# A four-layer network on one core: loading the next pair's first rows ahead, spacing the norm chains, and adding the last residual on VectorE

## The chip, the core and the metric

The kernel runs on one core of a Trainium2 chip. Its engines run side by side, each through its own list of instructions, and wait for one another by semaphores: TensorE (PE) multiplies matrices into PSUM, VectorE (DVE) and ScalarE (ACT) compute elementwise, GpSimd (POOL) does small work and issues DMAs, and SyncE (SP) issues nearly all DMAs. The metric is the device time of one execution in microseconds (us); lower is better.

## The reference

The input has 8 images of 64 channels and 128 x 128 pixels, all float32. Four layers follow, each a residual around a group-normalized input:

```python
x = x + _L0_conv_ref(_gn(x), L0_conv_w, L0_conv_b)
x = x + _L1_conv_ref(_gn(x), L1_conv_coef, L1_conv_scale_base, L1_conv_scale_sp, L1_conv_bias)
x = x + _L2_conv_ref(_gn(x), L2_conv_dw_w, L2_conv_dw_b, L2_conv_pw_w, L2_conv_pw_b, L2_conv_cv_w, L2_conv_cv_b)
x = x + _L3_conv_ref(_gn(x), L3_conv_embed_weight)
```

- `_gn` subtracts the mean and divides by the deviation over groups of 2 channels, for each image.
- Layer 0, the adder layer: each of 64 outputs is `relu(b - sum(|patch - w|))` over the 576 values of a 3 x 3 patch.
- Layer 1, the spline layer: per channel, `scale_base * silu(x) + scale_sp * spline(x) + bias`.
- Layer 2, the wavelet layer: a Haar transform, depthwise 3 x 3, 1 x 1 and 3 x 3 convolutions, an exact GELU, and the inverse transform.
- Layer 3, the quantizer: each pixel's 64 channels are replaced by the nearest of 512 code vectors.

## The kernel before, in words

Images are worked on in four pairs; the two images' channels fill the 128 partitions. A program that orders the instructions of every engine by its own estimate of time stands between this source and the engines; inside the adder layer the order on TensorE, ScalarE and VectorE is the one written.

**Adder layer** (`layer0`, L479 on). The image is cut into 4 chunks of 32 rows (`RA`), the 64 outputs into 4 groups of 16: 16 parts `p` for a pair. For each output the nine taps are computed as 128 x 4096 tiles `buf`: kind A by one ScalarE activation (L594), D by one VectorE operation (L596), C and T by further VectorE operations on the same buffer (L600), which cover two or three taps. TensorE sums every tile over the channels with eight matmuls (L663). Which kinds make up an output is written in `PLANS`, by what else runs beside. The tile buffers form a ring (`free`), 8 in the first pair and 7 later; one of them holds the chunk of x with a border (`load`, L506; normalized in place by `pad`, L518). Tiles are computed ahead as far as buffers are free. Two tiles are a *step*; `chores` lists what else is done at a step: channel sums and their way through DRAM (L537 to L559), the ReLU (`relu`, L568), the residual, which is eight DMAs of GpSimd that add x in flight (`residual`, L578), then statistics and eight stores (`finish`, L582).

**Beside it**: during the adder layer of pair n, layers 2 and 3 of pair n-1 are computed (`layer2_beside`, L941; `layer3_beside`, L1097), and in the last two parts the statistics of the next pair's input (`raw_stats`, L397). These are generators; each `yield` is a step. Layer 2 and layer 3 list their events by step number; layer 2 has 452 steps beside parts 0 to 7, layer 3 has 396 beside parts 8 to 13.

**Spline layer** (`layer1`, L670 on). It has no other layer beside it. A unit is 8 rows; `twice` (L683) loads it so that both halves of the partitions hold one image (`xd`). The per-channel scales `sb` and `zb` (L700 to L707) come from the layer's `mr` and the weights `l1w`.

**Normalization** (`group_norm_steps`, L427). `mr` holds mean and reciprocal deviation. Statistics are aggregated by VectorE (L458, L459), summed over channel pairs by a small matmul (L436, called at L460), used by VectorE for the variance (L462 to L466), summed again (L467), and turned into the reciprocal root by GpSimd (L471). `group_norm` (L418) runs the chain through at once: in front of the adder layer for the next input and for layer 2, and, with `by_tile`, between adder and spline layer. In layer 3 it runs at steps 0, 2 and 4 (L1176).

**Between layers.** At the end of the spline layer of a pair, `run` (L1194) first does the chain of the next input and that of layer 2, then enters `layer0`, which loads and normalizes its first chunk (`load(0)`, `pad(0)`, L638). At the end of the adder layer the ReLU of part 15 is followed by GpSimd's residual, the statistics, the chain, and the spline layer's scales. The last pair has no other beside its layers 2 and 3, which follow one after the other.

Of the kernel before, what the change touches and what calls it, by code (L numbers as in the profile page):

```python
# [21 lines left out]
P = 128  # L22
# [4 lines left out]
RA = 32  # L27
# [73 lines left out]
class Net:  # L101
# [295 lines left out]
    def raw_stats(self, pair, stats):  # L397

        with self.tc.tile_pool(name="raw", bufs=3) as pool:
            for j in range(NCH):  # L400
                t = pool.tile([P, R * W], F32, name="raw")
                self.nc.sync.dma_start(out=t, in_=self.x_dram[pair][:, j * R * W : (j + 1) * R * W])
                yield
                self.tile_stats(stats, 4 * j, t)
                yield

# [11 lines left out]
    def group_norm(self, stats, by_tile=False):  # L418


        with self.tc.tile_pool(name="gn_ps", bufs=1, space=PSUM) as pp:
            mr = self.small.tile([P, 2], F32, name="mr", tag="mr", bufs=4)
            for _ in self.group_norm_steps(stats, mr, pp, by_tile):
                pass
        return mr

    def group_norm_steps(self, stats, mr, pp, by_tile=False):  # L427
# [6 lines left out]
        def product(lhsT, rhs):  # L434
            t = pp.tile([P, 2 * NG], F32, name="gn", tag="gn")
            nc.tensor.matmul(t[:, 0 : rhs.shape[1]], lhsT, rhs, start=True, stop=True)  # L436
            return t
# [21 lines left out]
        nc.vector.tensor_reduce(total, mv[:, :, 0], AX.X, ALU.add)  # L459
        pm = product(self.pair, total)  # L460
# [5 lines left out]
        nc.vector.tensor_reduce(total, dv, AX.X, ALU.add)  # L466
        pv = product(self.pair, total)  # L467
# [10 lines left out]

    def layer0(self, pair, mr, stats, bufs, beside):  # L479

# [7 lines left out]
        with ExitStack() as ctx:  # L488
# [4 lines left out]
            free = deque(bp.tile([P, (RA + 2) * (W + 2)], F32, name=f"buf{n}") for n in range(bufs))  # L493
            held, xps, pss, sums, sxs, sts, ys = {}, {}, {}, {}, {}, {}, {}
            plan = [beside(p)[0] for p in range(NP)]

            def rows(j):

                lo, hi = max(j * RA - 1, 0), min((j + 1) * RA + 1, H)
                return lo, hi, xps[j][:, lo - j * RA + 1 : hi - j * RA + 1, 1 : W + 1]  # L500
# [5 lines left out]
            def load(j):  # L506
                held[j] = free.popleft()
                xp = xps[j] = held[j].rearrange("p (r w) -> p r w", w=W + 2)
                nc.gpsimd.memset(xp[:, :, 0:1], 0.0)
                nc.gpsimd.memset(xp[:, :, W + 1 : W + 2], 0.0)  # L510
                if j == 0:
                    nc.gpsimd.memset(xp[:, 0, 1 : W + 1], 0.0)
                if (j + 1) * RA == H:
                    nc.gpsimd.memset(xp[:, RA + 1, 1 : W + 1], 0.0)
                lo, hi, at = rows(j)
                nc.sync.dma_start(out=at, in_=x_in[:, lo * W : hi * W].rearrange("p (r w) -> p r w", w=W))

            def pad(j):  # L518
                at = rows(j)[2]
                self.normalize(at, at, mr)  # L520
# [57 lines left out]
            def residual(p, n):  # L578
                at, d = list(by_tile(x_in, p))[n]
                nc.gpsimd.dma_start(out=ys[p][at], in_=d, accum_op=ALU.add)  # L580

            def finish(p):  # L582
                j, o = divmod(p, OG)
                self.tile_stats(stats, NCH * 4 // OG * o + 2 * j, ys[p].rearrange("p q n -> p (q n)"))
                for at, d in by_tile(self.x_of[0], p):
                    nc.sync.dma_start(out=d, in_=ys[p][at])
# [27 lines left out]
            for p in range(NP):  # L614
                begin, end = first[p] // 2, first[p + 1] // 2
                j = p // OG
                if p % OG == 0:
                    for at, f, *a in (
                        (begin - 24, load),
                        (begin - 8, pad),  # L620
                        *[(begin + 5 + 4 * h, sum_channels, h) for h in range(3)],
                        *[(begin + 7 + 4 * h, take_sums, h) for h in range(3)],
                        *[(begin + 17 + t, shift, t) for t in range(FIRST_MAX, 9)],
                    ):
                        chores[at].append((f, j, *a))
                for at, f, *a in (
                    (begin + (40 if p % OG == 0 else 12), linear),
                    (end, relu),
                    *[(end + 2 + n, residual, n) for n in range(8)],
                    (end + 14, finish),  # L630
                ):
                    chores[at].append((f, p, *a))
                steps, count = beside(p)[1:]
                for n in range(begin, end):
                    k = n - begin
                    for _ in range((k + 1) * count // (end - begin) - k * count // (end - begin)):
                        chores[n].append((next, steps, None))
            load(0)  # L638
            pad(0)
# [30 lines left out]
    def layer1(self, mr, stats, store):  # L670
# [3 lines left out]
        with ExitStack() as ctx:  # L674
# [34 lines left out]
            def end(n, pa, pb):  # L709
# [7 lines left out]
                if n % 2 == 1:  # L717
                    j = n // 2
                    self.chunk_stats(stats, j)
                    if store:  # L720
                        nc.sync.dma_start(out=self.x_of[1][:, j * R * W : (j + 1) * R * W], in_=self.x[j].rearrange("p r w -> p (r w)"))

            late = None
            for n in range(2 * NCH):
# [39 lines left out]
                late = (n, pa, pb)  # L764
                if n + 3 < 2 * NCH:
                    xds.append(twice(n + 3))
                if n in range(4, 12, 2) and not store:
# [173 lines left out]
    def layer2_beside(self, mr, stats, steps):  # L941
# [13 lines left out]
        with ExitStack() as ctx:  # L955
            sp = ctx.enter_context(tc.tile_pool(name="b2", bufs=1))
            pp = ctx.enter_context(tc.tile_pool(name="b2_ps", bufs=1, space=PSUM))
            dws = sp.tile([P, 4, 9], F32, name="dws")
            nc.vector.tensor_scalar(dws, self.dww, mr[:, 1:2], 0.5, ALU.mult, ALU.mult)
            m4 = sp.tile([P, 1], F32, name="m4")  # L960
            nc.vector.tensor_scalar(m4, mr[:, 0:1], -4.0, None, ALU.mult)
# [87 lines left out]
            def inverse(j, pos):  # L1049
                py = pys[j, pos] = pp.tile([P, G, S], F32, name="py", bufs=2)  # L1050
# [12 lines left out]

            for j in range(NCH + 1):
                b, each = (0, LEAD) if j == 0 else (LEAD + EACH * (j - 1), EACH)
# [31 lines left out]
    def layer3_beside(self, stats, pair, steps):  # L1097
# [8 lines left out]
        with ExitStack() as ctx:  # L1106
# [3 lines left out]
            mr = self.small.tile([P, 2], F32, name="mr", tag="mr", bufs=4)  # L1110
# [65 lines left out]
            for n in range(3):  # L1176
                at(2 * n, next, norm)
            for j in range(NCH):
                b = 16 + EACH * j
# [14 lines left out]
    def run(self):  # L1194
        tc = self.tc
        stats = self.stats_tile()
        for _ in self.raw_stats(0, stats):
            pass
        later = None
        for pair in range(self.n_pairs):  # L1200
            last = pair + 1 == self.n_pairs
            mr, stats, nxt = self.group_norm(stats), self.stats_tile(), self.stats_tile()
            raw, count = (iter(()), 1) if last else (self.raw_stats(pair + 1, nxt), 2 * NCH + 1)
            if later is None:
                self.layer0(pair, mr, stats, BUFS_ALONE, lambda p: (0, raw, (count + 1) // 2 if p >= NP - 2 else 0))
            else:
                with tc.tile_pool(name="between", bufs=1) as bp:
                    between = bp.tile([P, NCH * 4, 6], F32, name="between")
                    plans = [3] + [1] * 7 + [2] * 6 + [0] * 2
                    counts = [TILES[n] // 2 for n in plans[:-2]]  # L1210
                    steps = chain(self.layer2_beside(later, between, sum(counts[:8])), self.layer3_beside(between, pair - 1, sum(counts[8:])), raw)
                    counts += [(count + 1) // 2] * 2
                    self.layer0(pair, mr, stats, BUFS_BESIDE, lambda p: (plans[p], steps, counts[p]))
            with tc.tile_pool(name="x", bufs=NCH if last else 3) as self.xpool, ExitStack() as ctx:
                if last:
                    self.w2 = ctx.enter_context(tc.tile_pool(name="w2", bufs=1)).tile([P, 4, 9, 2, P], F32, name="w2")
                mr, stats = self.group_norm(stats, by_tile=True), self.stats_tile()
                self.layer1(mr, stats, not last)
                later = self.group_norm(stats)
                if last:  # L1220
                    stats = self.stats_tile()
                    self.layer2(later, stats)
                    ctx.close()
                    self.layer3(self.group_norm(stats), pair)
            stats = nxt
# [33 lines left out]
```

## Time and profile before

| | us |
|---|---|
| median of 3 runs | 19377.96 (19377.81 to 19379.85) |
| profiled execution, its own time | 19381.0 |
| span of its profile | 19379.3 |
| TensorE's granted clock in it, mean | 0.976 |
| adder layer of the first pair, first to last matmul L663 | 143.03 to 3785.2 |
| spline layer of the first pair, first to last matmul | 3809.2 to 4049.35 |
| adder layer of the second pair, first matmul | 4071.70 |
| spline layer of the second pair, first activation | 8555.95 |
| last pair alone: layer 2 and 3 after the spline layer | 18295.9 to 19379.3 |

A row of the timeline has the start within the span, the duration, the engine, the line in the source, the operation, what is written from what, how many such instructions were merged, and in brackets how long the engine stood idle before and what ended that. SPq is SyncE's issuing of DMAs: the time shown there is that of the issue, not of the transfer. Matmuls overlap, so a busy TensorE is not one at its peak.

### The profile page before, as it was taken

To read this page: it belongs to the slowest core of one execution; us is meant where nothing else is said; L and a number is where in the kernel's file an instruction comes from. 1 tells how busy PE (TensorE), PEld (TensorE's weight loads), DVE (VectorE), ACT (ScalarE), POOL (GpSimd) and SP (SyncE) were. 2 spreads that over 40 slices of the span, in tenths; PEclk is the share of its full clock that TensorE was granted. 3 is DMA by queue.
4 is the path that set the end of the run, shared out by engine and by line. 5 is a ranking of instruction groups with operands and counts; after the bars stand their busy time and mean duration, and the time that the engine had idled before them with its cause. 6 is when DMAs were issued, how large, how long until landed. Compare 5 with 4: busy or idle time off the path is not lost. (4 is left out here: it accounts for less than half of the span.)

```text
span 19379.3 us, 328672 instructions
## 1 busy us (share of the span) xinstructions
PE 18590.2 (96%) x145850; PEld 5787.0 (30%) x145850; DVE 17864.6 (92%) x13781; ACT 17303.9 (89%) x6401; POOL 2828.8 (15%) x1730
## 2 busy tenths in 40 slices
PE   8999999999999999999999999999999999999898
PEld 2333333232222222222222222222222322222343
DVE  8999999989999999988999999998899989999837
ACT  7999999889999999988999999998899999999603
POOL 0000000000000344200000034420000004441005
PEclk9999999999999999999999999999999999999996
DMA  1000000111101000021111100002111110000201
GB/s 52 6 11 10 6 12 8 49 58 36 41 28 34 20 21 25 26 71 38 34 41 34 32 15 24 24 27 78 36 32 37 35 31 17 24 22 15 58 1 35
DMA packets 412641, 584.04 MB, mean 30 GB/s; under 512 B 64080, under 2 KB 309456, under 8 KB 385744
## 3 DMA queue, kind: packets, MB, share of 16 engines
q1 hardware_dynamic: 353872, 495.80, 8.5%
q0 software_dynamic: 57344, 67.21, 2.0%
q8 instruction: 1142, 18.71, 0.4%
q14 instruction: 283, 2.32, 0.0%
HBM read 439.55 MB, written 123.25 MB: 29 GB/s over the span
## 5 line engine op out<-in xcount | busy, mean ns | idle before, releaser
L594 ACT ACTIVATE buf<-buf,w 128x4096 f32<-128x4096 f32 x4314 | 15670.0, 3709 | 848.3 <-PE ps L663 713.3
L663 PE MATMUL ps<-buf,sel 128*32 128x512 f32 x127168 | 14115.4, 598 | 412.5 <-DVE buf L600 222.5
L596 DVE TENSOR_SCALAR buf<-buf,w 128x4096 f32<-128x4096 f32 x3634 | 8433.1, 2361 | 594.9 <-PE ps L663 589.2
L663 PEld LDWEIGHTS ps<-buf,sel 128*32 128x32 f32 x127168 | 3986.6, 110 | 10233.9 <-issue 8654.0
L600 DVE SCALAR_TENSOR_TENSOR buf<-buf,w,buf 128x2048 f32<-128x2048 f32 x2536 | 5855.1, 2349 | 46.3
L1155 POOL DMA_INDIRECT g<-in_L_conv_embed_weight,ix x768 | 1876.4, 2443 | 2753.1 <-issue 1151.8
L580 POOL DMA_DIRECT2D y<-in_x x512 | 634.1, 2007 | 10145.2 <-ACT y L568 8143.3
L1030 PE MATMUL cv<-dw,w2s 64*128 64x512 f32 x6912 | 1652.7, 607 | 23.8 <-DVE dw L1011 12.3
L1030 PEld LDWEIGHTS cv<-dw,w2s 64*128 64x128 f32 x6912 | 626.1, 186 | 1047.8 <-issue 1044.2
L1007 DVE SCALAR_TENSOR_TENSOR dw<-sub,dws,dw 128x512 f32<-128x512 f32 (+2 forms) x768 | 574.8, 748 | 10.1
L843 PE MATMUL ps<-dw,w 64*128 64x512 f32 x2304 | 525.2, 597 | 30.4 <-DVE dw L829 20.1
L1152 DVE CUSTOM_DVE_ANT_0 nd<-pd,t 128x512 f32<-128x512 f32 x768 | 520.1, 677 | 19.2 <-ACT t L1142 18.6
L1154 DVE FIND_INDEX8 ix<-best,nd 128x8 uint32<-128x512 f32 x768 | 526.2, 685 | 0.1
L748 DVE TENSOR_TENSOR r<-r,r 128x1024 f32<-128x1024 f32 x384 | 455.5, 1219 | 76.3 <-ACT r L747 76.2
L1142 ACT ACTIVATE t<-esq_half,xsq 128x512 f32<-128x512 f32 x768 | 509.6, 714 | 1.5 <-DVE best L1152 1.5
L1140 PE MATMUL pd<-embT,xn 64*128 64x512 f32 x1536 | 482.5, 644 | 29.0 <-DVE best L1152 29.0
L849 ACT ACTIVATE g<-ps,b2c 128x1024 f32<-128x1024 f32 x16 | 17.8, 1115 | 517.7 <-PE ps L843 517.7
L747 ACT ACTIVATE r<-r 128x1024 f32<-128x1024 f32 x384 | 385.3, 1045 | 93.3 <-PE pb L759 70.0
L759 PE MATMUL pa<-r,l1w 128*64 128x512 f32 x1536 | 425.8, 609 | 26.8 <-DVE r L748 26.8
L759 PE MATMUL pb<-r,l1w 128*64 128x512 f32 x1536 | 418.2, 597 | 0.0
L911 ACT ACTIVATE t<-esq_half,xsq 128x512 f32<-128x512 f32 x256 | 171.4, 714 | 242.7 <-DVE best L914 205.2
L843 PEld LDWEIGHTS ps<-dw,w 64*128 64x128 f32 x2304 | 239.9, 188 | 305.2 <-issue 269.6
(206 smaller groups left out, 5292.0 us busy)
## 6 DMA issues: line engine op xcount, KB each, us to landing
w2s<-w_dram SPq DMA_DIRECT2D x576, 192.0 KB
xd<-x_dram SPq DMA_DIRECT2D x256, 256.0 KB
x<-x_dram SPq DMA_DIRECT2D x56, 1024.0 KB
raw<-in_x SPq DMA_DIRECT2D x32, 1024.0 KB
y<-in_x POOLq DMA_DIRECT2D x512, 64.0 KB, 4.2
x_dram<-y SPq DMA_DIRECT2D x512, 64.0 KB
out<-x SPq DMA_DIRECT2D x32, 1024.0 KB
x_dram<-x SPq DMA_DIRECT2D x24, 1024.0 KB
```

What stands on the lines that cost most here:

```text
L580: nc.gpsimd.dma_start(out=ys[p][at], in_=d, accum_op=ALU.add)
L594: nc.scalar.activation(ab, tap(j, ts[0]), AF.Abs, bias=w[:, ts[0] : ts[0] + 1], scale=-1.0)
L596: nc.vector.tensor_scalar(ab, tap(j, ts[0]), w[:, ts[0] : ts[0] + 1], None, ALU.max)
L600: nc.vector.scalar_tensor_tensor(at, tap(j, t, h), w[:, t : t + 1], at, ALU.max, ALU.add)
L663: nc.tensor.matmul(at, sel[:, M - 1 - m : 3 * M - 1 - m], rhs, start=(n == first[p]), stop=(n + 1 == first[p + 1]))
L759: nc.tensor.matmul(to[images[i], q, :], dspl[:, k, ws[i], :], cubes[i][:, cols], start=(p == 0), stop=stop)
L843: nc.tensor.matmul(ps[:, i], self.w2[rows, k, w, oab, :], v, start=(n == 0 and k == 0), stop=(n == 8 and k == 3))
L1007: nc.vector.scalar_tensor_tensor(out, v, wt, out, ALU.mult, ALU.add)
L1030: nc.tensor.matmul(ps[:, i], weights[r, w // 3, :], v, start=(k == 0 and n == 0), stop=(k == 3 and n == 8))
L1152: nc.vector.tensor_tensor_reduce(nd, ps, t, 1.0, -FAR, ALU.subtract, ALU.max, mx[:, 0:1])
L1154: nc.vector.max_index(ix, mx, nd)
L1155: nc.gpsimd.indirect_dma_start(out=g[:, img, :], out_offset=None, in_=self.embed, in_offset=bass.IndirectOffsetOnAxis(ap=ix[:, 0:1], axis=0),)
```

## The change

- **First rows ahead.** The first chunk of x of a pair gets a tile of its own, `x0`, outside the ring's pool; the ring has one buffer less and takes `x0` in when the chunk is used up. For the first pair it is loaded after the raw tiles. For a later pair it is loaded right after the adder layer of the pair before, and normalized inside the spline layer between (`pad_first`).
- **Chains in steps.** The raw statistics and their chain become one generator, `raw_norm`, in the last two parts (24 steps of it, not 17). The chain of layer 2 runs in layer 2's first seven steps, and all its other events come seven steps later. The chain of layer 3 runs at steps 0 to 6, and its rows begin one step later. In the chain, two more `yield`s stand ahead of each small matmul.
- **Last residual.** For part 15, x is loaded by SyncE into a free ring buffer one step before the part ends, and VectorE adds it.

```diff
-    def raw_stats(self, pair, stats):
+    def raw_norm(self, pair, mr):
+        stats = self.stats_tile()
         with self.tc.tile_pool(name="raw", bufs=3) as pool:
...
+        with self.tc.tile_pool(name="raw_ps", bufs=1, space=PSUM) as pp:
+            yield from self.group_norm_steps(stats, mr, pp)
...
         nc.vector.tensor_reduce(total, mv[:, :, 0], AX.X, ALU.add)
+        yield
+        yield
         pm = product(self.pair, total)
...
         nc.vector.tensor_reduce(total, dv, AX.X, ALU.add)
+        yield
+        yield
         pv = product(self.pair, total)
...
+    def pad_first(self, mr):
+        at = self.chunk_rows(self.x0.rearrange("p (r w) -> p r w", w=W + 2), 0)[2]
+        self.normalize(at, at, mr)
...
             def residual(p, n):
                 at, d = list(by_tile(x_in, p))[n]
-                nc.gpsimd.dma_start(out=ys[p][at], in_=d, accum_op=ALU.add)
+                if p + 1 < NP:
+                    nc.gpsimd.dma_start(out=ys[p][at], in_=d, accum_op=ALU.add)
+                    return
+                if n == 0:
+                    xr.append(free.popleft()[:, 0 : 2 * NE].rearrange("p (q n) -> p q n", q=2))
+                nc.sync.dma_start(out=xr[0][at], in_=d)
 
             def finish(p):
                 j, o = divmod(p, OG)
+                if p + 1 == NP:
+                    nc.vector.tensor_tensor(ys[p], ys[p], xr[0], ALU.add)
...
-                    *[(end + 2 + n, residual, n) for n in range(8)],
-                    (end + 14, finish),
+                    *[(end + 2 + n if p + 1 < NP else end - 1, residual, n) for n in range(8)],
+                    (end + (14 if p + 1 < NP else 0), finish),
...
-            load(0)
-            pad(0)
+            held[0] = self.x0
+            xps[0] = self.x0.rearrange("p (r w) -> p r w", w=W + 2)
...
+                if n == 4 and nxt is not None:
+                    self.pad_first(nxt)
...
+            for n in range(7):
+                at(n, next, norm)
+            at(8, scales)
             for j in range(NCH + 1):
-                b, each = (0, LEAD) if j == 0 else (LEAD + EACH * (j - 1), EACH)
+                b, each = (7, LEAD) if j == 0 else (7 + LEAD + EACH * (j - 1), EACH)
...
-            for n in range(3):
-                at(2 * n, next, norm)
+            for n in range(7):
+                at(n, next, norm)
             for j in range(NCH):
-                b = 16 + EACH * j
+                b = 17 + EACH * j
...
                 if last:
+                    first.close()
+                else:
+                    self.load_chunk(pair + 1, 0, self.x0)
+                with tc.tile_pool(name="x", bufs=NCH if last else 3) as self.xpool, ExitStack() as ctx:
...
+                    mr, later = self.group_norm(stats, by_tile=True), self.stats_tile()
+                    self.layer1(mr, later, None if last else nxt)
```

## The prediction

> **What bounds the kernel now.** I read the page's busy shares first, then the groups, then the places where TensorE stands still.
>
> ```profile
> PE 18590.2 (96%) x145850; PEld 5787.0 (30%) x145850; DVE 17864.6 (92%) x13781; ACT 17303.9 (89%) x6401; POOL 2828.8 (15%) x1730
> ...
> L594 ACT ACTIVATE buf<-buf,w 128x4096 f32<-128x4096 f32 x4314 | 15670.0, 3709 | 848.3 <-PE ps L663 713.3
> L663 PE MATMUL ps<-buf,sel 128*32 128x512 f32 x127168 | 14115.4, 598 | 412.5 <-DVE buf L600 222.5
> ```
>
> Three engines are busy 89% or more: the adder layer is balanced, and no single engine can be relieved alone. ScalarE's idle time there mostly ends with a matmul (713.3 us), that of the matmuls with VectorE. So time comes only from places where all of them wait. Adding up the gaps between matmuls that exceed 3 us gives 326 us; most lie at the stage borders. The change touches four kinds of them, shown in order of time.
>
> Border from the spline layer to the next pair's adder layer, by the timeline (start, duration, engine, line):
>
> ```profile
> 4050.70 0.32 SPq L721 DMA_DIRECT2D x_dram<-x  x1
> ...
> 4054.86 0.67 SPq L516 DMA_DIRECT2D buf<-in_x  x1
> ...
> 4065.16 2.54 DVE L475 TENSOR_SCALAR buf<-buf,mr 128x4224 f32<-128x4224 f32 x1 [6.34 <-DMA buf<-in_x]
> ...
> 4067.94 18.15 ACT L594 ACTIVATE buf<-buf,w 128x4096 f32<-128x4096 f32 x5 [29.97 <-issue]
> 4071.70 13.86 PE L663 MATMUL ps<-buf,sel 128*32 128x512 f32 x112 [13.08 <-ACT buf L594]
> ```
>
> The first rows are asked for only when the spline layer's last store has landed (4050.70 to 4054.86), take 10.3 us, are normalized for 2.54 us, and only then do ScalarE and VectorE begin. The two normalization chains between (4052.0 to 4058.9) lie under that load and cost nothing.
>
> Border from adder to spline layer:
>
> ```profile
> 3785.24 1.11 ACT L568 ACTIVATE y<-ps,b 128x1024 f32<-128x1024 f32 x1 [13.30 <-PE ps L663]
> ...
> 3786.65 6.45 POOL L580 DMA_DIRECT2D y<-in_x  x8 [219.52 <-ACT y L568]
> ...
> 3795.74 1.28 DVE L413 BATCH_NORM_STATS2 stats<-y 128x6 f32<-128x512 f32 x2 [14.95 <-DMA y<-in_x]
> ...
> 3803.40 1.24 ACT L735 ACTIVATE z<-xd,zb 128x1024 f32<-128x1024 f32 x1 [17.04 <-DVE zb L707]
> ```
>
> Call E the end of the last adder matmul (3785.2). The residual holds the sums back until E+10.6; the spline layer starts at E+18.2.
>
> Start of the quantizer (layer 3) beside the adder layer: the timeline, and two rows of the busy table by stretch (from:to, length, busy us of PE, PEld, DVE, ACT, POOL, then the granted clock):
>
> ```profile
> 6386.21 0.56 PE L436 MATMUL gn<-total,pair 128*128 128x1 f32 x2 [4.67 <-DVE total L459]
> ...
> 6401.20 0.59 PE L436 MATMUL gn<-total,pair 128*128 128x1 f32 x2 [4.47 <-DVE total L466]
> ```
>
> ```profile
> 6380.00:6412.00 32.00, 22.38 (x152) 6.27 (x156) 17.84 (x15) 22.22 (x8) 6.45 (x8) 0.73 0.19 33
> 6412.00:8000.00 1588.00, 1553.17 (x12944) 461.40 (x12940) 1534.70 (x1572) 1568.81 (x659) 673.61 (x295) 0.99 0.08 20
> ```
>
> TensorE's queue stands twice for a sum that VectorE makes only after tiles that it computes ahead. ScalarE is busy 98.8% afterwards, so its idle time here is lost for good.
>
> **The opening.** The last raw load is issued at 116.3, the first rows' load at 126.41 (when the raw tiles' memory is free), and normalization starts at 136.63, though the scale was there at 130.9. With memory of its own the load follows the raw ones at once: by the 7.6 us that its packets take at 4056, it ends near 130, and the scale ends last. **Gain 5.5 us.**
>
> **Spline to adder layer, three times.** Load and normalization are gone from here. What is late next: the first ScalarE buffer lies where the spline layer's last x tile was, so it still waits for that store, until 4054.9. VectorE's first buffers lie elsewhere and can start after the statistics, near 4052. ScalarE moves from 4067.94 to 4054.9: **13.0 us each, 39.0.** Ends: 10 if VectorE's buffers wait too and the start is ragged, 15.5 if the store isn't waited for.
>
> **Quantizer start, three times.** With the spacing, the sum's matmul stands four tiles later, behind six tiles of the stage instead of two, and VectorE has the sum about when the sixth tile is through. ScalarE was busy 22.2 of 32 us; at 98.8% it would be 31.6: 9.4 us lost. I leave about 1 us for a remaining wait: **8.5 each, 25.5.** Here a rule and a row give different sums. The Trainium skill (TensorE: Matmul & The Clock Gate, section "What's actually happening") says that the array falls to half clock after an idle window of about 3.4 us. The clock row shows it: 0.73 in these 32 us. By the rule, gaps (9.1 us) plus half-clock work (some 17 us at half speed, 8 us) would be worth 17 us per pair. By the row it is 9.4, because ScalarE, not TensorE, is the bound behind it. I take the row.
>
> **Adder to spline layer, four times.** Removed: eight accumulating DMAs by GpSimd. Added: eight loads on SP's queue into a borrowed buffer, and one VectorE add. In the changed program's order that buffer is last read six tiles before E in the first pair, five in the others; a tile is 0.88 us (160 matmuls in 17.56 us). Loads go from E-5.3 (E-4.4), issue for 3.9 us in all (eight stores took 4.37), and the last lands some 2.9 us later (a row load: issued 4091.64, used 4094.55), at E+1.5 (E+2.4). Behind these loads' wait SP holds only what comes after E. The add costs 1.22 us (row L748), so the sums start at E+2.8 (E+3.7) rather than E+10.6: up to 7.8 (6.9) us. In the last pair nothing else changes: **6.9.**
>
> In the others the next pair's first rows (2.16 MB) are loaded here, and on SP's queue this load stands before the eight result stores, the spline weights and the first xd loads. Before, weights and two xd loads were issued at E+0.2. Their new place waits on the stores. The Trainium skill (DMA: Bandwidth & Descriptors, section "Queues, rings and completion order") says that SP owns one row of rings, and that an engine consumes descriptors in ring order. It speaks against this change; the trace agrees where it can: around 3797 to 3804 packets of an xd load, of an x load and of the next xd loads follow one another in issue order. By the rule, the rows' packets occupy the ring until E+7.7 (E+8.6), stores another 3.2 us, weights 1.7 (1 MB takes 3.3 us in the opening), two xd loads 1.7, landing 1.2: the spline layer starts at E+15.5, **2.7 earlier, in the first pair.** In the two middle ones a 1 MB x load stands before the weights too: E+19.7, **1.5 later, twice.** By the VectorE chain alone all would gain 6.9 to 7.8. The 2.54 us normalization stands in VectorE's program before the spline scales; a late load would hold VectorE and everything behind it, but the weights come later still. Sum of this border **6.6**; ends -8 and 26.
>
> **What is added elsewhere.** The raw chain's VectorE part (1.02 for the aggregate and seven steps near 0.16) moves into the last tiles, where VectorE is the busiest (8000 to 8536: 524 of 536): **-2.2, three times, -6.6.** The layer-2 chain moves into the first steps, where VectorE has room (4072 to 4230: 133 of 158): nothing. Layer 2 begins seven steps later, and its third row load now stands on SP's queue behind the channel-sum stores and gathers; VectorE may wait some 7 us for it while ScalarE has buffers left: I take **-2 each, -6**, ends 0 and -7. The shift also moves seven steps of layer 2 from the roomy first tile into the last one before the quantizer (VectorE 79.65 of 80 us busy before 6380): about six us of VectorE work per pair; TensorE gains there what VectorE loses. I take 0, ends -6 and 3 per pair. GpSimd loses 32 DMAs and sets the row borders (0.7 us) at another time: idle anyway.
>
> Sum: 5.5 + 39.0 + 25.5 + 6.6 - 6.6 - 6.0 = 64.0. The profiled execution took 19381.0 (span 19379.3), the median of the runs 19377.96; 64 less is 19317 and **19314**.
>
> **Rivals.** (1) The queue is no obstacle: the small transfers slip past the big load, the late row load finds VectorE idle anyhow. Then the adder border gives 28 and the minus 6 falls away: 64 + 21 + 6 = 91, 19287. For: nothing in the old trace has such a load before urgent ones; against: packets in issue order. (2) The quantizer's stall only moves: the six tiles' buffers run out anyway, or the sum is late again. Minus 25.5: 19340. For: VectorE made tiles ahead before the sum, and still does; against: the matmul now stands behind those tiles. (3) Slower: the seven-step shift. If the last tile before the quantizer and the tiles with layer 2 are VectorE-bound, depthwise work that had room now stretches every pair. It decides from 21 us per pair, more than three times the 6 us that I count as moved; at 30 us per pair the sum is 64 - 90, so 19404. For: VectorE is at 99% there; against: the layer's total is unchanged, and its last step (449 of 452) still fits.
>
> **Chances.** Forecast 0.63 (19290 to 19338), rival 1 0.20, rival 2 0.13, rival 3 0.04. No change means within 0.2%, 39 us, about what can be told here. Faster: 0.62 + 0.20 + 0.07 = 0.89; same 0.01 + 0.06; slower 0.04. The range, 19272 to 19344, takes in rival 1 and half of rival 2.
>
> **What will show it.** First adder matmul of a later pair 9.4 us after the last spline matmul instead of 22.4; no TensorE gap above 2 us on the sum's matmul at the quantizer; first spline activation at E+15.5, E+19.7, E+19.7 and E+11.3; first adder activation at 133.7. Wrong if the first x tile's buffer waits for more than the store, if the first spline activation waits for the normalization of the next pair's rows, or if VectorE waits on xin for more than 7 us in each first tile.

## The result, and the profile after

| | before | after |
|---|---|---|
| median of 4 runs, us | 19378.9 (19377.81 to 19386.12) | 19249.67 (19248.76 to 19257.7) |
| span of the profile, us | 19379.3 | 19247.0 |

The ratio is 0.9933, with a 95% interval from 0.9921 to 0.9946: 129 us less, where 64 were forecast, and below the range. The page of the changed kernel, its busy line and then three of its groups (busy us, mean ns | idle time before, and what ended it):

```profile
PE 18582.4 (97%) x145850; PEld 5795.2 (30%) x145850; DVE 17869.9 (93%) x13785; ACT 17302.3 (90%) x6401; POOL 2775.6 (14%) x1698
...
L691 PE MATMUL ps<-buf,sel 128*32 128x512 f32 x116336 | 13032.1, 598 | 358.4 <-DVE buf L628 233.4
L622 ACT ACTIVATE buf<-buf,w 128x4096 f32<-128x4096 f32 x1980 | 7212.9, 3708 | 305.9 <-PE ps L691 299.5
L622 ACT ACTIVATE buf<-x,w 128x4096 f32<-128x4096 f32 x1938 | 7044.5, 3708 | 376.5 <-PE ps L691 290.8
...
L622 ACT ACTIVATE x<-buf,w 128x4096 f32<-128x4096 f32 x396 | 1468.6, 3709 | 60.8 <-PE ps L691 60.7
```

TensorE, VectorE and ScalarE have as much to do as before, within 8 us. The tile called `x` is `x0`, which has a name of its own now and splits the old group of ScalarE in three: their idle time is 743 us together, where it was 848.3. Waiting has gone, not work.

Where it went, from the first and last matmuls of each stage and the ReLUs of the parts (forecast by the terms of the prediction's sum; the changes add up to -132.2, that of the profile's span):

| us | change | forecast |
|---|---|---|
| opening | -5.8 | -5.5 |
| three borders spline to adder layer (TensorE's gap, 66.4 to 27.3) | -39.1 | -39.0 |
| four borders adder to spline layer, to the first large spline matmul (97.6 to 77.8; to the first activation, as forecast, 73.4 to 56.6, -16.8) | -19.8 | -6.6 |
| pairs 2 to 4, parts 0 to 7 (layer 2 beside) | -36.4 | +6.0 |
| pairs 2 to 4, parts 8 to 13 (quantizer beside) | -26.9 | -25.5 |
| parts 14 and 15, and all of the first pair's adder layer | +1.9 | +6.6 |
| the four spline layers | -1.3 | 0 |
| the last pair's layers 2 and 3 | -5.0 | 0 |

The last two rows are hardly the change's: in the kernels below, the stretch of the last row takes 1079 to 1085 us (before 1083.4, after 1078.4), and a spline layer moves by up to 3 us either way.

The timeline at the first border from spline to adder layer (start, duration, engine, line, and in brackets the idle time before):

```profile
4043.54 0.32 SPq L749 DMA_DIRECT2D x_dram<-x  x1
...
4047.51 10.93 ACT L622 ACTIVATE buf<-x,w 128x4096 f32<-128x4096 f32 x3 [16.70 <-DMA x_dram<-x]
4047.80 6.96 DVE L624 TENSOR_SCALAR buf<-x,w 128x4096 f32<-128x4096 f32 x3 [2.96 <-DMA x_dram<-x]
...
4051.28 5.27 PE L691 MATMUL ps<-buf,sel 128*32 128x512 f32 x24 [9.09 <-ACT buf L622]
```

Load and normalization are gone, and ScalarE waits for the store, as forecast. VectorE waits for it too.

The quantizer's start, the two products of its chain in the timeline, and then the busy table of the 32 us around them (from:to, length, busy us of PE, PEld, DVE, ACT, POOL, granted clock):

```profile
6360.22 0.38 PE L442 MATMUL gn<-total,pair 128*128 128x1 f32 x2
...
6371.63 0.38 PE L442 MATMUL gn<-total,pair 128*128 128x1 f32 x2
```

```profile
6348.00:6380.00 32.00, 29.19 (x272) 8.76 (x268) 31.46 (x22) 32.00 (x11) 16.38 (x9) 1.00 0.34 86
```

No bracket: TensorE no longer stands before either. ScalarE is busy 32.0 us of 32, where it was 22.2, and the clock is 1.00, where it was 0.73.

The second border from adder to spline layer. The last adder matmul ends at 8497.67 (E):

```profile
8488.30 3.61 SPq L606 DMA_DIRECT2D buf<-in_x  x8
8492.01 0.67 SPq L500 DMA_DIRECT2D x<-in_x  x1
...
8500.13 3.58 SPq L614 DMA_DIRECT2D x_dram<-y  x8
...
8503.82 0.36 SPq L394 DMA_DIRECT2D x<-x_dram  x1
...
8505.40 0.34 SPq L722 DMA_DIRECT2D l1w<-l1w_dram  x1
...
8505.79 10.85 SPq L716 DMA_DIRECT2D xd<-x_dram  x12
...
8513.23 0.98 PE L734 MATMUL pm<-sb,l1w 128*128 128x2 f32 x4 [7.51 <-DMA xd<-x_dram]
...
8514.28 1.24 ACT L763 ACTIVATE z<-xd,zb 128x1024 f32<-128x1024 f32 x1 [1.28 <-DMA xd<-x_dram]
```

The residual's loads go at E-9.4, the next pair's first rows at E-5.7, ahead of E. The scales `sb` are ready at 8509; the weights and xd, asked for only at E+7.7 and E+8.1, come near E+16. This border is set by loads now, not by the chain. The first activation stands at E+12.6, 16.6, 17.2 and 10.2 in the four pairs (before: 18.2, 18.1, 18.1, 19.0; forecast: 15.5, 19.7, 19.7, 11.3).

### The profile page after: what moved, and what is told of

It is laid out like the page before. It is cut to its first block, busy times and chain, and to the rows that moved or that the text cites. A ratio compares the mean times of both kernels' runs of the same rounds, so it can differ in the third digit from the quotient of the medians.

```text
span 19247.0 us, 328577 instructions
## 1 busy us (share of the span) xinstructions
PE 18582.4 (97%) x145850; PEld 5795.2 (30%) x145850; DVE 17869.9 (93%) x13785; ACT 17302.3 (90%) x6401; POOL 2775.6 (14%) x1698
## 4 chain that ended last, share of the span: by engine, by line
PE 54%; DVE 27%; issue 9%; ACT 8%; DMA 1%; POOL 0%; SPq 0%; DVEq 0%; ACTq 0%; POOLq 0%
PE ps L691 39%; DVE buf L624 12%; DVE buf L628 9%; ACT buf L622 7%; PE cv L1066 5%; PE pa L787 2%; PE pb L787 2%; PE ps L873 2%; DVE dw L1043 1%; DVE ix L1193 1%; DVE nd L1191 1%; PE ps L938 1%; DVE x L624 1%; PE py L1089 1%; PE pd L1179 1%
## 5 line engine op out<-in xcount | busy, mean ns | idle before, releaser
L691 PE MATMUL ps<-buf,sel 128*32 128x512 f32 x116336 | 13032.1, 598 | 358.4 <-DVE buf L628 233.4
L622 ACT ACTIVATE buf<-buf,w 128x4096 f32<-128x4096 f32 x1980 | 7212.9, 3708 | 305.9 <-PE ps L691 299.5
L622 ACT ACTIVATE buf<-x,w 128x4096 f32<-128x4096 f32 x1938 | 7044.5, 3708 | 376.5 <-PE ps L691 290.8
L624 DVE TENSOR_SCALAR buf<-buf,w 128x4096 f32<-128x4096 f32 x1795 | 4162.7, 2357 | 193.7 <-PE ps L691 192.9
L624 DVE TENSOR_SCALAR buf<-x,w 128x4096 f32<-128x4096 f32 x1558 | 3640.1, 2367 | 284.3 <-PE ps L691 274.5
L628 DVE SCALAR_TENSOR_TENSOR buf<-buf,w,buf 128x2048 f32<-128x2048 f32 x1262 | 2913.5, 2349 | 23.0
L628 DVE SCALAR_TENSOR_TENSOR buf<-x,w,buf 128x2048 f32<-128x2048 f32 x1072 | 2475.3, 2349 | 19.7
L622 ACT ACTIVATE x<-buf,w 128x4096 f32<-128x4096 f32 x396 | 1468.6, 3709 | 60.8 <-PE ps L691 60.7
L691 PE MATMUL ps<-x,sel 128*32 128x512 f32 x10832 | 1302.8, 595 | 27.1 <-DVE x L628 18.9
L624 DVE TENSOR_SCALAR x<-buf,w 128x4096 f32<-128x4096 f32 x281 | 660.2, 2349 | 24.4 <-PE ps L691 24.2
L873 PE MATMUL ps<-dw,w 64*128 64x512 f32 x2304 | 525.5, 597 | 29.4 <-DVE dw L859 20.4
```

What stands on the lines that cost most here:

```text
L622: nc.scalar.activation(ab, tap(j, ts[0]), AF.Abs, bias=w[:, ts[0] : ts[0] + 1], scale=-1.0)
L624: nc.vector.tensor_scalar(ab, tap(j, ts[0]), w[:, ts[0] : ts[0] + 1], None, ALU.max)
L628: nc.vector.scalar_tensor_tensor(at, tap(j, t, h), w[:, t : t + 1], at, ALU.max, ALU.add)
L691: nc.tensor.matmul(at, sel[:, M - 1 - m : 3 * M - 1 - m], rhs, start=(n == first[p]), stop=(n + 1 == first[p + 1]))
L873: nc.tensor.matmul(ps[:, i], self.w2[rows, k, w, oab, :], v, start=(n == 0 and k == 0), stop=(n == 8 and k == 3))
```

## The experiments

Two terms were far off: layer 2's later start, and the border from adder to spline layer. Times below are of one run each unless said otherwise. Runs of the changed kernel lay up to 9 us apart and nine runs of the kernel before up to 16, so smaller differences aren't read from the time of one run; the lengths of single parts, from the profile, repeat within 3 us. The expectations count pairs from 0, the text from the first.

**The quantizer's chain as before** (`l3_old`; `wide=False` leaves out the two added `yield`s ahead of each small matmul):

```diff
-norm = self.group_norm_steps(stats, mr, pq)
+norm = self.group_norm_steps(stats, mr, pq, wide=False)
...
-for n in range(7):
-    at(n, next, norm)
+for n in range(3):
+    at(2 * n, next, norm)
-    b = 17 + EACH * j
+    b = 16 + EACH * j
```

> The changed kernel with the quantizer's chain as it was (steps 0, 2, 4, no extra yields, rows from step 16). Theory A, the stall at the quantizer's start is worth 15 to 17 us a pair (gaps and slow TensorE work together), so parts 8 and 9 grow by 13 to 17 us a pair, parts 0 to 7 stay within 2, time about 19295 (+45 to +51 on the changed kernel). Theory B, the price on record, 8.5 a pair holds and the rest comes from layer 2's later start: +25, about 19275. Theory C, parts 8 and 9 are shorter because of layer 2's later end, not of the chain: under +10, 19250 to 19258.

19275.34: 8.6 us a pair by the time, which fits theory B. The parts show more. Parts 8 and 9 are 15 to 20 us a pair longer than in the changed kernel, as theory A had it or more, and parts 10 to 13 together some 7 shorter; parts 8 to 13 of the three pairs are 32 us longer in sum, parts 0 to 7 are not. The run `l3_b16` below takes the two apart.

**Layer 2's chain at the border, with and without the later events** (`l2_border`, `l2_border_noshift`):

```diff
+later = self.group_norm(later)
...
-for n in range(7):
-    at(n, next, norm)
-at(8, scales)
+scales()
...
-b, each = (7, LEAD) if j == 0 else (7 + LEAD + EACH * (j - 1), EACH)
+b, each = (0, LEAD) if j == 0 else (LEAD + EACH * (j - 1), EACH)
```

The last pair of lines is in `l2_border_noshift` only.

> The changed kernel with layer 2's chain back at the border, all of layer 2's events still seven steps late. If the later events alone shorten parts 0 to 7, these parts stay as in the changed kernel (within 2 us a pair) and only the border is dearer: ScalarE still waits for the store until 5.3 us after the spline layer's last matmul, VectorE starts about 7 us later than it could, 0 to 7 us a pair, time 19248 to 19270. If it is the chain's place that shortens them, parts 0 to 7 grow back by about 10 us a pair: 19277 to 19290.

> As the run before, and layer 2's events at their old steps too: only the spline borders, the quantizer's chain, the raw chain and the last residual are changed. If the seven steps are what shortens parts 0 to 7, these parts are back at the kernel before (within 3 us a pair; 10 to 16 us a pair longer than in the changed kernel), and 19280 to 19310. If they cost nothing, as the prediction on record took it, the time is within 10 us of the run with the shift alone kept, and parts 0 to 7 are short in both.

19256.13 and 19291.94. The border is 9.1 us long in both, as in the changed kernel: taking the chain from it was worth nothing that shows (the 6 us between 19256 and 19250 are within the scatter). The seven steps alone are worth 35.8 us by the time. In parts 0 to 7 of the three pairs, against the kernel before: +5.0 us without them, -34.3 with them. This is the term that had been priced at nothing.

**Why? The trace at one place.** In the second pair, the border of layer 2's sixth block comes due near step 278. The timeline before:

```profile
5477.62 4.62 DVE L600 SCALAR_TENSOR_TENSOR buf<-buf,w,buf 128x2048 f32<-128x2048 f32 x2
5482.15 0.42 DVE L1011 COPY dw<-dw 128x512 f32<-128x512 f32 x1
5482.86 2.85 PE L1030 MATMUL cv<-dw,w2s 64*128 64x512 f32 x12 [3.53 <-DVE dw L1011]
...
5487.75 2.35 DVE L596 TENSOR_SCALAR buf<-buf,w 128x4096 f32<-128x4096 f32 x1 [5.18 <-PE ps L663]
...
5497.74 7.32 ACT L594 ACTIVATE buf<-buf,w 128x4096 f32<-128x4096 f32 x2 [4.00 <-PE ps L663]
```

The same work after:

```profile
5486.37 25.36 ACT L622 ACTIVATE buf<-buf,w 128x4096 f32<-128x4096 f32 x7
5486.40 0.42 DVE L1047 COPY dw<-dw 128x512 f32<-128x512 f32 x1
...
5489.11 4.62 DVE L628 SCALAR_TENSOR_TENSOR buf<-buf,w,buf 128x2048 f32<-128x2048 f32 x2
5491.99 2.85 PE L1066 MATMUL cv<-dw,w2s 64*128 64x512 f32 x12
```

Before, VectorE first finishes a tile of 7 us that it computes ahead, and copies the border row (L1011) after it. TensorE's list holds the first convolution matmul of the block (L1030) there and waits 3.5 us; with it wait the matmuls that would set tile buffers free, so VectorE then stands for 5.2 us and ScalarE for 4.0. It is the quantizer's stall in another place. After, the copy comes ahead of the tile, and nobody waits for it. The busy tables of a stretch around this copy, before and then after (columns as above; the stretches differ in length):

```profile
5475.70:5503.80 28.10, 24.57 (x184) 8.16 (x179) 22.78 (x15) 24.10 (x8) 0.00 (x0) 1.00 0.05 15
```

```profile
5475.60:5512.90 37.30, 35.28 (x278) 10.70 (x271) 37.13 (x24) 37.30 (x13) 0.00 (x0) 1.00 0.07 19
```

ScalarE: 24.1 of 28.1 us, then 37.3 of 37.3. Over the whole run, the view of the tile `cv` lists what the engines that work on it waited for (us, times). Before, `l2_border_noshift`, and `l2_border`:

```profile
its engine sat idle before it (us, times) until:
  issue: 1078.8, 2963
  DVE dw L1011: 12.3, 4
```

```profile
its engine sat idle before it (us, times) until:
  issue: 1090.1, 2962
  DVE dw L1045: 15.9, 6
```

```profile
its engine sat idle before it (us, times) until:
  issue: 1037.4, 2941
  ACT buf L622: 5.0, 3
  ACT x L622: 3.2, 2
  DMA st<-s_dram: 2.4, 3
```

The waits for the copied row are there before and without the seven steps, and not with them. The view puts only part of the waiting down to the copy. Counted from the trace, TensorE's gaps of over 0.3 us ahead of these matmuls are 23.6 us in the kernel before, 31.1 without the seven steps and 3.2 with them, and each of them ends 0.1 to 0.3 us after such a copy. That is 28 us less, where parts 0 to 7 lose 39.

**Later, or merely elsewhere?** (`shift3`, `shift9`: the number in `b, each` is 3 or 9, the chain is at the border as in `l2_border`.)

> Layer 2's chain at the border, its events 3 steps late instead of 7 (the run with 7 took 19256, with none 19292). If lateness as such helps (say, the ring of tile buffers fills before layer 2's first work comes), parts 0 to 7 lie between, with part 0 shorter and the others as with none: 19272 to 19282. If it is how layer 2's bunches of work fall on the ends of the adder layer's parts, a pattern that repeats with every part, the gain is scattered over parts with both signs and doesn't follow the number of steps: anywhere from 19250 to 19310, and single parts change by 3 to 8 us.

> The same with 9 steps, the most that fits. If lateness as such helps: 19245 to 19256, all parts near those with 7. If it is how the bunches fall on the parts' ends: anywhere from 19240 to 19310, with parts that change by 3 to 8 us against the run with 7.

19264.36 and 19249.76: with 0, 3, 7 and 9 steps the time falls, 19292, 19264, 19256, 19250, which looks like lateness. The parts say otherwise. In sum, parts 0 to 7 of the three pairs change by +5, -32, -34 and -37 us, so three steps bring nearly all of it. Their lengths in the fourth pair, against the kernel before, us:

| part | 0 | 1 | 2 | 3 | 4 | 5 | 6 | 7 |
|---|---|---|---|---|---|---|---|---|
| no steps | 0.0 | 0.0 | -1.1 | +3.2 | +2.7 | 0.0 | 0.0 | +0.1 |
| 3 steps | +0.1 | -1.9 | -3.3 | -3.0 | -3.2 | +5.5 | -0.1 | -1.6 |
| 7 steps | -4.0 | +0.3 | -3.8 | +1.1 | -2.4 | -5.8 | +6.7 | -3.1 |
| 9 steps | -6.8 | +3.0 | -1.3 | -2.9 | -2.3 | -5.2 | +6.9 | -1.4 |

Both signs, and part 5 is 5.5 longer with 3 steps and 5.8 shorter with 7; with 3 steps the one gap left ahead of the convolution matmuls, 4.5 us in every pair, lies in this part. The rows for 7 and 9 steps are much alike, so `shift9` decides little. To tell the two apart, the order of the tiles was changed instead of layer 2 (`rotated`, without the seven steps, and `rotated_late`, with them; the chain is at the border in both):

```diff
+PLANS = PLANS[:1] + (PLANS[1][4:] + PLANS[1][:4],) + PLANS[2:]
```

> The run without the seven steps (19292), with the eight patterns of tile kinds of parts 1 to 7 begun at the fifth: the same tiles and work in another order. If what counts is how layer 2's bunches fall on the adder layer's tiles, single parts from 1 to 7 change by 3 to 8 us, both ways, and the sum by up to 12 us a pair: 19260 to 19320. If it is the lateness of layer 2, parts 1 to 7 change by under 2 us each: 19285 to 19298.

> The same rotated patterns with layer 2's events seven steps late. If lateness as such is worth 12 us a pair, this is again 30 to 42 us faster than the rotated run without it. If it is how the bunches fall on the tiles, the difference is another one, anything from 20 us faster to 20 us slower, and the parts that gain are others than 0, 2, 5 and 7.

19277.0 and 19275.7: with the patterns rotated, the seven steps are worth 1 us in the time of single runs, where they were worth 36. The parts make it sharper. Parts 1 to 7 of the three pairs together gain 27.5 us from the seven steps with the old patterns, and 0.1 with the rotated ones. Part 0, whose patterns were not rotated, gains 4 us a pair in both. And the rotation alone, with layer 2 at its old steps, shortens parts 1 to 7 by 27 us; in the time 15 of them are left, since parts 8 to 13 grow by 15, and by 5 more with the seven steps. The view of `cv` in `rotated`, without the seven steps:

```profile
its engine sat idle before it (us, times) until:
  issue: 1060.9, 2957
  ACT buf L623: 5.0, 3
  DMA x_dram<-y: 0.8, 1
```

The waits put down to the copied row are gone here too; the gaps ahead of these matmuls are 8.0 us, where they were 31.1 with the old patterns, and none in `rotated_late`. So in parts 1 to 7 it is how layer 2's due work falls on the tiles computed ahead, not lateness. The gaps don't account for every part: part 6 is 6.7 us longer with 7 steps, with a gap of 1.1. And part 0's 12 us in all stay unexplained: they come with seven steps under either order and not with three, so lateness isn't ruled out there.

**One step in the quantizer** (`l3_b16`; `quant_b16` is the same kernel in five runs): the chain stays in steps 0 to 6, and the rows begin at step 16 as before.

```diff
-    b = 17 + EACH * j
+    b = 16 + EACH * j
```

> The changed kernel with the quantizer's chain still in steps 0 to 6, but its rows from step 16 as before, not 17. If parts 10 to 13 are longer in the changed kernel because the rows come one step later (+6.8 us a pair there), that is gone here and parts 8 and 9 keep their gain: about 19230 (19227 to 19238). If the spaced chain itself costs the 6.8, or the earlier rows bring the stall at the start back, parts 8 to 13 sum to the same or more: 19248 to 19265.

> The run with the quantizer's spaced chain and its rows from step 16 once more, in five rounds. One look gave 19240.0; if the spacing is worth 11.8 us a pair and the one step of delay costs 3.2, the median lies at 19236 to 19244. If that look was a lucky one within the scatter of single runs, it is 19245 to 19252.

19239.97, and in five runs 19240.09 (19237.33 to 19242.42; 0.9928 of the kernel before, which took 19380.1 beside it; interval 0.9915 to 0.9942). That is below every run of the changed kernel. Part 13, 6.8 us longer in the changed kernel, is back within 2.2 us of the kernel before, while about 3 us a pair of part 9's gain are lost. Against `l3_old`, which has the same rows, the spaced chain is worth 35.3 us by the time, 11.8 a pair, and 42 by the lengths of parts 8 to 13, 14 a pair; the one step of delay that came with it costs 9.6 by either, 3.2 a pair. The lengths, which repeat, are the better measure of the two. The forecast 8.5 was near the net of the two, not near either.

**The border from adder to spline layer.** First the residual by GpSimd again (`res_old`):

```diff
-if p + 1 < NP:
-    nc.gpsimd.dma_start(out=ys[p][at], in_=d, accum_op=ALU.add)
-    return
...
-nc.sync.dma_start(out=xr[0][at], in_=d)
+nc.gpsimd.dma_start(out=ys[p][at], in_=d, accum_op=ALU.add)
...
-if p + 1 == NP:
-    nc.vector.tensor_tensor(ys[p], ys[p], xr[0], ALU.add)
...
-*[(end + 2 + n if p + 1 < NP else end - 1, residual, n) for n in range(8)],
-(end + (14 if p + 1 < NP else 0), finish),
+*[(end + 2 + n, residual, n) for n in range(8)],
+(end + 14, finish),
```

> The changed kernel with the last residual by GpSimd again, twelve steps before the sums are complete, all else as changed. In pairs 1 and 2 the weights' load then stands behind all eight stores, which stand behind GpSimd's eight transfers: the first spline activation comes at 20 to 25 us after the last adder matmul there, at 16 to 19 in pair 0 and 18.5 to 19.5 in pair 3, 21 to 31 us more in all than in the changed kernel: 19268 to 19284. If the residual was hidden anyway, all stay within 2 us of the changed kernel: 19245 to 19256.

19281.64, 32 us slower. The timeline of the second border there; E is 8509.01:

```profile
8510.49 8.42 POOL L601 DMA_DIRECT2D y<-in_x  x8 [5.77 <-ACT y L589]
...
8516.72 5.37 SPq L607 DMA_DIRECT2D x_dram<-y  x8
8521.09 1.29 DVE L419 BATCH_NORM_STATS2 stats<-y 128x6 f32<-128x512 f32 x2 [6.13 <-DMA y<-in_x]
...
8523.77 0.34 SPq L715 DMA_DIRECT2D l1w<-l1w_dram  x1
...
8532.88 1.24 ACT L756 ACTIVATE z<-xd,zb 128x1024 f32<-128x1024 f32 x1 [1.32 <-DMA xd<-x_dram]
```

The first activation comes at E+20.4, 23.9, 25.3 and 18.7: 88.3 us in sum, 56.6 in the changed kernel, 73.4 before. So the residual part is worth 31.7 us, and the rest of the change costs 15 of them back, 13 at the second and third border: there the weights were asked for at E+0.2 before, ahead of the stores on SP's queue, and come behind them now.

Then the first rows' load put behind the spline layer's first loads in the source (`x0_late`), and with it the small weights of `zb` kept from the program's start and the first rows' normalization held back to unit 4 (`border2`):

```diff
 xds = [twice(n) for n in range(3)]
+if nxt is not None:
+    self.load_chunk(nxt_pair, 0, self.x0)
...
-else:
-    self.load_chunk(pair + 1, 0, self.x0)
```

```diff
+self.nc.sync.dma_start(out=self.image_w, in_=self.l1w_dram[:, 12 * C :])
...
+nc.vector.scalar_tensor_tensor(mn, self.x[1][:, 0, 0:2], 0.0, nxt, ALU.mult, ALU.add)
-self.pad_first(nxt)
+self.pad_first(mn)
```

> The changed kernel with the first rows of the next pair asked for after the spline layer's first loads, not ahead of the last stores. If the big transfer holds up the loads that come after it on the rings (the reading on record), the first spline activation of pairs 1 and 2 comes 3 to 5 us earlier than at 16.6 and 17.2 us after the last adder matmul, pair 0 by 0 to 3, time about 19238 to 19244. If the weights' load there only waits for the stores and the x tile ahead of it, the activation stays within 1 us: 19244 to 19252.

> The changed kernel with three things at the border from adder to spline layer: first rows asked for after the spline layer's first loads, the small weights for zb kept from the start of the program, and the first rows' normalization held until unit 4 has begun. Theory, the late l1w (landed 7.5 us after its issue, behind the x tile) and the normalization ahead of zb are what hold the activation: it comes at 9.5 to 10.5 us after the last adder matmul in pair 0 and 11 to 13.5 in pairs 1 and 2 (12.6, 16.6, 17.2 in the changed kernel), and the time is 6 to 12 below the run with the late rows alone (19242.6): 19231 to 19237. Rival, the xd tiles land no earlier than zb did, so that only pair 0 gains: 19238 to 19243.

`x0_late` took 19242.61, but its activations stand where they were, at E+12.6, 16.7 and 16.9. The trace shows why: the edit moved nothing. SyncE's issues at the second border in `x0_late` (E is 8490.76):

```profile
8485.10 0.67 SPq L500 DMA_DIRECT2D x<-in_x  x1
8493.23 3.11 SPq L614 DMA_DIRECT2D x_dram<-y  x7
```

The rows are asked for at E-5.7, as in the changed kernel; `border2` has them there too (8499.22, E 8504.87): the program that orders the instructions put the load back ahead of the stores, and all of SyncE's DMAs stand in the same order in `x0_late` as in the changed kernel. So `x0_late` says nothing on the rows' load, and its 7 us lie within the scatter. A comparison within the changed kernel answers the question: the last pair loads no rows there, and its stores' packets run from E+3.3 to E+7.3, at the second border too. The rows don't hold the stores up.

`border2` took 19260.25, a miss. Its other two edits did take hold: E+12.5, 15.7, 16.0, so `zb` and the normalization together held the activation by no more than 1.2 us in the changed kernel, and the spline layers, with the normalization in their middle, are up to 4 us longer. Last, the memory: the spline layer's pools opened in another order, so that weights and xd lie elsewhere, not where `y` does (`pools_first`):

```diff
-sp = ctx.enter_context(tc.tile_pool(name="l1", bufs=2))
-xdp = ctx.enter_context(tc.tile_pool(name="l1_xd", bufs=3))
 cp = ctx.enter_context(tc.tile_pool(name="l1_c", bufs=1))
+xdp = ctx.enter_context(tc.tile_pool(name="l1_xd", bufs=3))
+sp = ctx.enter_context(tc.tile_pool(name="l1", bufs=2))
```

> The changed kernel with the spline layer's pools opened in another order (weights and xd tiles first), so that they lie elsewhere in memory; nothing else. Theory, at the border from adder to spline layer of pairs 1 and 2 the weights and xd tiles wait for the last stores only because they lie where y lies, and behind the x tile: the first activation comes at 12 to 13.5 us after the last adder matmul, not 16.6 and 17.2, pair 0 stays at 12 to 13, about 8 us less in all: 19238 to 19245. Rival, the xd tiles wait for what the stores write, or for the rings: still above 16, 19246 to 19254.

19251.01: no gain in all. Pairs 2 and 3 gained as the theory had it (E+14.1 and 12.5, not 16.6 and 17.2), but pair 4, which nobody had thought of, lost 7. Its border in that kernel; E is 17903.14:

```profile
17905.60 3.57 SPq L614 DMA_DIRECT2D x_dram<-y  x8
...
17909.34 0.34 SPq L722 DMA_DIRECT2D l1w<-l1w_dram  x1
...
17910.85 10.58 SPq L716 DMA_DIRECT2D xd<-x_dram  x12
...
17920.30 1.23 ACT L763 ACTIVATE z<-xd,zb 128x1024 f32<-128x1024 f32 x1
```

In the changed kernel the last pair's weights were asked for at 15777 and its first xd at 17446, long before E; in the new layout both come only after E, like the others. Only the place in memory was changed, so the wait for memory that is still in use is the likely cause at these three borders.

**Both gains together** (`combined`, five runs): rows from step 16, and layer 2 nine steps late with its chain in steps.

```diff
-b, each = (7, LEAD) if j == 0 else (7 + LEAD + EACH * (j - 1), EACH)
+b, each = (9, LEAD) if j == 0 else (9 + LEAD + EACH * (j - 1), EACH)
...
-    b = 17 + EACH * j
+    b = 16 + EACH * j
```

> The same with layer 2's events nine steps late instead of seven (its chain in steps, as in the changed kernel). With the chain at the border nine steps were 6.4 us faster than seven; if the two add up, 19231 to 19238; if not, the same as with seven, 19238 to 19246.

19235.61 (19231.61 to 19240.33; 0.9927 of the kernel before, interval 0.9913 to 0.994). All five runs lie below all runs of the changed kernel, by 14 us in the median. Against `quant_b16` the ranges overlap, so the nine steps' own share isn't shown.

## Why the prediction was wrong

The direction and three of the terms were right; the sum was short by half, and one step made most of that.

- **The step that failed: "The shift also moves seven steps of layer 2 ... I take 0, ends -6 and 3 per pair", and with it "-2 each, -6" for the late row load.** Together +6.0 were forecast for parts 0 to 7, and -36.4 came: 42 of the 68 us by which the gain of the profile's span exceeded the forecast. The step counted how much VectorE work moves from a roomy tile to a full one, and never asked which waits of TensorE inside layer 2 depend on the order. They were in the old trace, in the view of `cv` and at 5482.86 in the timeline; the prediction counted gaps at the borders and at the quantizer alone. VectorE did wait longer for the row loads (`xin`: 1.6 us before, 12.4 after), as feared, but part 0 became 3.6 to 4.1 us shorter all the same. Rival 3 had the place, with the wrong sign. That rival 1's time, 19287, lay nearer than the forecast is luck: its six us at the late row load did not come as it said, since VectorE waited longer there.
- **The border from adder to spline layer, 6.6 forecast, 16.8 measured at the first activation (19.8 at the first large matmul).** That the weights wait for the stores was right; the mis-sized step is the moment at which the borrowed buffer is free. The residual's loads were to go at E-5.3 (E-4.4) and went at E-11.1 (E-9.4), and the rows behind them at E-7.4 (E-5.7). The Trainium skill's rule (DMA: Bandwidth & Descriptors, section "Queues, rings and completion order"), that descriptors are consumed in ring order, held: at the second border the packets of the rows, the stores, the x tile, the weights and xd follow one another in the trace in that order. But the rows' packets ran from 8493.5 to 8501.6, that is to E+3.9, where I had let them block until E+8.6; their 8.1 us were near the 7.6 forecast. They were nearly through when the stores were issued at E+2.5, and did not delay them. So rival 1 had this border's sign right, and its size (28) too large: loads still bind. For the last pair the forecast took 6.9 from the first pair's E+18.2; from its own 19.0 it would have been E+12.1, not 11.3, and 10.2 came.
- **The quantizer, 25.5 forecast, 26.9 measured in its parts and 25.7 by `l3_old`.** Right by compensation: the spacing gained 35 to 42, the delay by one step cost 9.6. The row (9.4 a pair) and the half-clock rule of the Trainium skill (TensorE: Matmul & The Clock Gate, section "What's actually happening"; 17, an estimate) enclose what came, 11.8 by the time and 14 by the parts. The clock did recover, 0.73 to 1.00. Over the 128 adder matmuls around the stall alone, in the second pair, `l3_b16` takes 17.5 us and `l3_old` 32.3: 14.9 less before rounding, nearer to the rule; 3 of it are gone by the end of the part.
- **Opening and the border from spline to adder layer: right to 0.3 us each.** That VectorE would start before the store had landed was wrong (it starts at 4047.80, after ScalarE) and cost nothing: TensorE's gap is 9.1 us, with 9.4 forecast.
- **The raw chain, -6.6 forecast:** parts 14 and 15 grew by 2.3 us in the first pair and by nothing in the others. Why the first pair pays more was not traced.

What stays open, besides part 0 above: why a step of delay costs the quantizer 6.8 us in part 13 was not traced; the collision with the tiles is likely, from what layer 2 shows, but not shown.

## What to carry to other kernels

Where two streams are woven into one in-order list per engine, look for every place where TensorE's list waits for a small VectorE result that stands behind tiles computed ahead; the wait costs all engines, and moving the small work by some steps, or reordering the tiles, can take it away at no cost in work. A constant shift isn't free by default: price it by the waits it makes or breaks, and try two or three values; here how late it was did not tell the best. After an edit, see in the trace that the instruction has moved: where a program orders the list, moving a line in the source may move nothing. And where one border waits for loads, look at what lies in the memory they go to: a new tile or pool elsewhere in the program can decide when they may start.

## What was not expected of the hardware

A load of 2.16 MB (packets of 5632 bytes) took 8.1 us at the second border, from its first packet to its last. And the same kernel moved by some us in single parts from run to run: in the two profiles of the kernel with rows from step 16, part 9 is 1.4 us shorter than before in the second pair of the one and 4.3 in that of the other, and the reverse in the third pair. A single run tells a part's change of 5 us, but not such a change of the whole.
